# Layer 0's attention: every PSUM bank gets a fixed purpose, and the preparation of the next group moves behind the outputs and denominators of a step

## The chip, the cores and the metric

The kernel runs on one core of one Trainium2 chip. The metric is device time in microseconds (us), the median over runs. The engines are called by their names in the profile: PE is TensorE's matmul (PEld its weight load), ACT is ScalarE, DVE is VectorE, POOL is GpSimd, SP issues most transfers.

## The reference, cut to what matters

The whole is a decoder of two layers over x (32 sequences, 128 tokens, width 256, float32). Layer 0 is a self-attention, a cross-attention to a context with distance slopes, and a mixture of eight experts; layer 1 is a gated recurrence with an MLP, a second cross-attention and a quantised feed-forward.

```python
x = x + attn(layernorm(x))            # 16 heads of 16; keys and values from a latent of 64
x = x + xattn(layernorm(x), ctx)      # 16 heads, scores + slope * (kpos - qpos), masked, softmax with +1
x = x + moe(layernorm(x))             # top 2 of 8 experts, 256 -> 1024 -> 256
x = x + layer1_mixer_and_mlp(layernorm(x))
x = x + layer1_xattn(layernorm(x), ctx)
x = x + layer1_ffn(layernorm(x))      # quantised 256 -> 1024, conv over tokens, silu, 1024 -> 256
```

## The kernel before, in words

The residual x stays in SBUF. Layer 0's attentions run in one function, attention(), over 64 items: item ("a", g, i) is the self-attention of sequence i of group g (8 groups of 4 sequences), item ("b", g, i) the cross-attention of the same. All "a" items come first, then all "b" items. Step t of the loop at L641 walks the list slots (L636) and issues pieces of several items:

- a_scores (s_a): 32 matmuls of 32 rows into four banks, then four DVE maxima into nm (L444), one for each bank. a_maxima: two transposes (bank nm_a) and one DVE add, qS (L455). a_weights, one step later: scores again, transposed, into four banks st_a, and four ACT exponentials (L474). a_outs, two steps late: outputs and denominators in one bank, od_a; DVE takes a reciprocal (L497) and a product. merge, three steps late: output projection in one bank, y_a, added to x (L506).
- b_scores (s_b): 16 matmuls into four banks; 16 DVE operations add slope and mask and take a running maximum (L518); two small DVE operations give nan, the negated maxima (L524, L525); 16 ACT exponentials (L531) need nan; DVE sums half of the denominators (L536); POOL spreads their reciprocals (L544). b_turned, two steps late: 16 transposes into four banks et_b, copied three by ACT and one by DVE (L555). b_outs three steps late (od_b), b_dens two steps late (rd_b, copied by ACT L565), merge four steps late.
- ahead: one piece of the preparation of the item's successor group, four pieces per group. For "a": layer norm and transposed x (pt_a, copied by ACT L291); queries and latent (q_a, l_a); keys (k_a, eight ACT operations L356); values (v_a, L317). For "b": loads, mask and keys (k_b, four ACT operations L313) with the layer norm; transposed x (pt_b); queries (q_b, L402); values (v_b, L317).
- route(g), after the last b item of a group: layer norm, transposed x (pt_c), router logits (r_c), top two.

PE's instructions in these functions go through mm and turned, which keep them in program order. The framework orders the other engines' instructions ahead of time, by program order among those that it takes to be ready[...].

PSUM has 8 banks. Every tile is a whole bank, from one pool of 8 buffers: a new tile gets any bank that is free. This pool serves the whole kernel, the experts and layer 1 too.

Layer 1 is a list of pieces by step: PLAN gives the step of each piece of a unit (two sequences), and each unit starts 11 steps after the one before, so that pieces of several units share a step. The pieces that matter below are e_s and e_exp (scores s_e, read by one DVE maximum L1212 and two ACT exponentials L1217), f_flip (pt_f and rows_f), e_flip (pt_e), m_fc (f_m) and f_h (h_f):

```python
(45, "e_s"), (47, "e_exp"), (58, "f_flip"), (60, "f_h0"), (13, "d_v d_q2"),
(26, "m_fc0 m_fc1"), (36, "e_flip"),
```

Of the kernel before, what the change touches and what calls it, by code (L numbers as in the profile page):

```python
# [2 lines left out]

# [7 lines left out]
F32 = mybir.dt.float32  # L11
# [6 lines left out]
P = 128  # L18
# [57 lines left out]
def decoder(ctx: ExitStack, tc: tile.TileContext, a: dict, out: bass.AP):  # L76
# [11 lines left out]
    psp = ctx.enter_context(tc.tile_pool(name="ps", bufs=8, space=bass.MemoryType.PSUM))  # L88

    def bank(name, dt=F32):  # L90
        return psp.tile([P, 512 if dt == F32 else 1024], dt, tag="ps", name=name)
# [153 lines left out]
    def attention():  # L245
        with tc.tile_pool(name="pa", bufs=2) as pool, tc.tile_pool(name="pa1", bufs=1) as keep:
# [38 lines left out]
            def xposed(src, name):  # L285
                dst = pool.tile([P, 2, GS], F32, tag="xT", name=f"xT_{name}")
                for c in range(2):
                    pt = bank(f"pt_{name}_{c}")
                    for i in range(G):
                        turned(pt[:, i * P : (i + 1) * P], src[:, i, c * P : (c + 1) * P])  # L290
                    A.copy(dst[:, c, :], pt)  # L291
                return dst

            def feats(w, m, xT, name, kc=2, msz=P, rows=P):
                p = bank(name)
                for c in range(kc):
                    mm(p[:msz, :GS], w[:rows, c, m * msz : (m + 1) * msz], xT[:rows, c, :], c == 0, c == kc - 1)
                return p

            def toks(w, xT, i, name, kc=2, rows=P):  # L300
                p = bank(name)
                for c in range(kc):
                    mm(p[:, :D], xT[:rows, c, i * S : (i + 1) * S], w[:rows, c, :], c == 0, c == kc - 1)
                return p

            def key_halves(w, xT, name):


                kEO = pool.tile([P, 2, G, 2, S], F32, tag="kEO", name=f"kEO_{name}")
                for c in range(2):  # L310
                    p = feats(w, c, xT, f"k_{name}_{c}").rearrange("p (b k) -> p b k", b=G)
                    for e in range(2):
                        A.activation(kEO[:, c, :, e, :], p, AF.Copy, scale=pm[:, e : e + 1])  # L313
                return kEO

# [5 lines left out]
            def group_a(g):  # L321
# [13 lines left out]
                p = bank(f"l_{n}")  # L335
# [9 lines left out]
                pk = [bank(f"k_{n}_{h}").rearrange("p (c b k) -> p c b k", c=2, b=2) for h in range(2)]  # L345
# [16 lines left out]
                pv_ = [bank(f"v_{n}_{h}").rearrange("p (i d) -> p i d", i=2) for h in range(2)]  # L362
# [9 lines left out]
            def group_b(g):  # L372
# [32 lines left out]
                v = vEO[g % 2]  # L405
                for i in range(G):
                    value_halves(v, toks(W("b_v", 2), cT, i, f"v_{n}_{i}"), i)
                made["b", g] = qT, kEO, v, nd

            def score(b, i, m):  # L410

                qT, kEO, _, _ = made[b[:2]]
                sp = [bank(f"s_{m}_{r}") for r in range(4)]
                if b[0] == "a":
                    for c in range(2):
                        for e in range(2):
                            for r in range(4):
                                at = slice(32 * r, 32 * r + 32)
                                mm(
                                    sp[r][:, (2 * c + e) * S : (2 * c + e + 1) * S],  # L420
                                    qT[at, c, e, i * S : (i + 1) * S], kEO[at, c, i, e, :], True, True,
                                )
                    return [s.rearrange("p (c e k) -> p c e k", c=2, e=2) for s in sp]
                for c in range(2):
                    for r in range(4):
                        mm(
                            sp[r][:, c * 2 * S : (c + 1) * 2 * S],
                            qT[32 * r : 32 * r + 32, c, i * S : (i + 1) * S],
                            kEO[32 * r : 32 * r + 32, c, i].rearrange("p e k -> p (e k)"),
                            True, True,  # L430
                        )
                return [s.rearrange("p (j k) -> p j k", j=4) for s in sp]
# [16 lines left out]
            def a_maxima(b):  # L449
                i, m = b[2], f"a{b[1]}_{b[2]}"  # L450
                pt = bank(f"nm_{m}")
# [10 lines left out]
            def a_weights(b):  # L462
                g, i, m = b[1], b[2], f"a{b[1]}_{b[2]}"
                kEO, qS = made[b[:2]][1], state[b]
                st = [bank(f"st_{m}_{r}") for r in range(4)]
# [26 lines left out]
            def a_outs(b):  # L492
                m = f"a{b[1]}_{b[2]}"
                od = bank(f"od_{m}")
# [7 lines left out]
            def merge(b):  # L502

                xg, i = X[b[1]], b[2]
                y = toks(W(f"{b[0]}_o", 2), state.pop(b), 0, f"y_{b[0]}{b[1]}_{i}")
                V.tensor_tensor(xg[:, i, :], xg[:, i, :], y[:, :D], ALU.add)  # L506
# [40 lines left out]
            def b_turned(b):  # L547
# [3 lines left out]
                for r in range(4):  # L551
                    pt = bank(f"et_{m}_{r}")
# [5 lines left out]
            def b_dens(b):  # L558
                m = f"b{b[1]}_{b[2]}"
                et, den = state[b]  # L560
                p = bank(f"rd_{m}")
# [6 lines left out]
            def b_outs(b):  # L568
                m = f"b{b[1]}_{b[2]}"
                od = bank(f"od_{m}")  # L570
# [5 lines left out]
            def route(g):  # L576
# [7 lines left out]
                xT = xposed(xn, n)  # L584
                yield
                p3 = bank(f"r_{n}")[:, : G * NE].rearrange("p (b e) -> p b e", b=G)
# [47 lines left out]
            for _ in group_a(0):  # L634
                pass
            slots = (  # L636
                (a_scores, 0), (b_scores, 0), (ahead, 0), (a_weights, 1), (b_turned, 2),
                (a_outs, 2), (b_outs, 3), (merge, None), (b_dens, 2), (a_maxima, 0),
            )
            routing = []  # L640
            for t in range(len(items) + 4):  # L641
                for what, late in slots:
                    if what is merge:
                        for late in (4, 3):
# [7 lines left out]
                routing = [r for r in routing if next(r, routing) is not routing]  # L652
# [820 lines left out]
```

## Time and profile before

| | us |
|---|---|
| median of three runs | 2037.29 (2035.19 to 2041.46) |
| the profiled execution: time | 2041.52 |
| its span | 2039.4 |
| self-attention items with preparation of "a" groups, 56.88 to 255.09 | 198.2 |
| cross-attention items, from 290.40 to about 621 | 331 |
| experts, 740 to 1340 | 600 |
| layer 1, from 1340 | 699 |

The profile is of one execution; its span is 2.1 us shorter than its time. PE is busy for 89% of the span, DVE for 57%, ACT for 53%; but these are averages over stages: in the experts' stage PE has no gap and the others idle, in the cross-attention PE, ACT and DVE are all busy for about four fifths of the time. A matmul of 32 rows lasts 270 ns in the profile, though one starts about every 30 ns, so PE's busy share covers short gaps; PE's stalls are read here from the distance between the starts of successive tiles.

### The profile page before, as it was taken

How to read it: one execution, taken by the hardware profiler on the slowest of the kernel's cores; microseconds unless marked ns; L12 is line 12 of the kernel's file. 1: busy time of each engine (PE TensorE's matmuls, PEld its weight loads, DVE VectorE, ACT ScalarE, POOL GpSimd, SP SyncE). 2: the span in 40 equal slices, each digit the busy share in tenths (PEclk: the TensorE clock that was granted, in tenths of full speed). 3: DMA queues.
4: the chain of work that ended last, by engine and by line, in shares of the span. 5: the costliest groups of instructions: out<-in, count | busy, mean ns of one | idle time of the engine just before them, and what ended most of it. 6: DMA issues, size and time to landing. Idle time of an engine off the chain costs nothing.

```text
span 2039.4 us, 35437 instructions
## 1 busy us (share of the span) xinstructions
PE 1807.9 (89%) x13432; PEld 1477.4 (72%) x13432; DVE 1166.9 (57%) x3716; ACT 1080.8 (53%) x2584; POOL 421.9 (21%) x445
## 2 busy tenths in 40 slices
PE   6999999899986799999999995379989999999863
PEld 4777766676665478888888885268878887888752
DVE  6877667787777512101111111454677888888787
ACT  4454548888885422222222221235677777777662
POOL 4100000000000111111111102852333333333221
PEclk8999999998998899999999998689999999999976
DMA  4000010111002845555546553310000000000000
GB/s 155 3 2 3 8 38 22 33 33 52 16 19 75 325 174 180 202 192 187 211 173 210 183 189 120 87 49 11 11 11 27 16 17 21 27 16 21 27 11 21
DMA packets 51517, 162.13 MB, mean 79 GB/s; under 512 B 5392, under 2 KB 32144, under 8 KB 46224
## 3 DMA queue, kind: packets, MB, share of 16 engines
q1 hardware_dynamic: 44816, 141.99, 19.6%
q0 software_dynamic: 6528, 17.83, 3.1%
q8 instruction: 108, 1.77, 0.4%
q14 instruction: 65, 0.53, 0.1%
HBM read 132.80 MB, written 27.00 MB: 78 GB/s over the span
## 4 chain that ended last, share of the span: by engine, by line
PE 51%; DVE 26%; ACT 10%; POOL 6%; issue 4%; DMA 3%; SPq 0%; POOLq 0%; DVEq 0%; ACTq 0%
PE h L206 12%; PE y L206 12%; ACT sd_b L531 4%; PE od_a L206 3%; DVE top_f L1311 3%; DVE sd_b L518 2%; POOL z_f L1298 2%; PE st_a L206 2%; PE m_m L206 2%; PE et_b L209 2%; PE f_m L206 1%; DMA yr<-ys,slots 1%; DVE rd_a L497 1%; DVE nm L444 1%; PE q_a L206 1%
## 5 line engine op out<-in xcount | busy, mean ns | idle before, releaser
L820 ACT ACTIVATE hTs<-h,moe 128x256 f32<-128x256 f32 x288 | 136.3, 473 | 374.5 <-PE h L206 374.5
L206 PE MATMUL h<-xTs,moe 128*128 128x256 f32 x1152 | 254.7, 379 | 1.0 <-issue 1.0
L206 PE MATMUL y<-moe,hTs 128*128 128x256 f32 x1152 | 254.6, 379 | 0.0
L206 PEld LDWEIGHTS h<-xTs,moe 128*128 128x128 f32 x1152 | 218.7, 190 | 30.9 <-issue 1.2
L206 PEld LDWEIGHTS y<-moe,hTs 128*128 128x128 f32 x1152 | 216.2, 190 | 27.9
L531 ACT ACTIVATE sd_b<-sd_b,nan_b 128x128 f32<-128x128 f32 x512 | 173.8, 387 | 28.9 <-DVE nan_b L525 28.7
L795 POOL DMA_INDIRECT xr<-xs,who x72 | 68.3, 948 | 469.6 <-PE xs L209 426.8
L808 DVE COPY xTs<-xs 128x512 f32<-128x512 f32 x36 | 24.9, 690 | 236.1 <-PE xs L209 236.1
L832 DVE TENSOR_TENSOR yt<-y,moe 128x256 f32<-128x256 f32 x72 | 30.5, 424 | 215.7 <-PE y L206 215.7
L206 PE MATMUL m_m<-wd,sT_m 128*128 128x256 f32 x512 | 119.4, 381 | 0.0
L206 PE MATMUL f_m<-hT_m,wd 128*128 128x256 f32 x512 | 116.9, 383 | 0.0
L518 DVE CUSTOM_DVE_ANT_0 sd_b<-nd_b,s_b 128x128 f32<-128x128 f32 x512 | 113.0, 278 | 5.4 <-PE s_b L206 5.4
L1298 POOL TENSOR_TENSOR z_f<-z_f,e_f 128x508 f32<-128x508 f32 x64 | 70.7, 1104 | 197.3 <-ACT e_f L1296 110.1
L206 PEld LDWEIGHTS f_m<-hT_m,wd 128*128 128x128 f32 x512 | 96.4, 193 | 12.9 <-issue 0.5
L206 PEld LDWEIGHTS m_m<-wd,sT_m 128*128 128x128 f32 x512 | 95.8, 192 | 12.6 <-ACT sT_m L1158 0.2
L497 DVE RECIPROCAL rd_a<-od_a 128x256 f32<-128x256 f32 x32 | 56.0, 1751 | 63.2 <-PE od_a L206 63.2
L1282 ACT ACTIVATE z_f<-d_f,pv 128x256 f32<-128x256 f32 x128 | 70.3, 590 | 35.7 <-DVE d_f L1277 35.6
L544 POOL COPY dens_b<-den_b 128x256 f32<-128x256 f32 x32 | 12.8, 399 | 363.6 <-DVE den_b L542 202.3
L1292 DVE SCALAR_TENSOR_TENSOR z_f<-d_f,pv,z_f 128x254 f32<-128x254 f32 x128 | 64.1, 509 | 37.6 <-ACT z_f L1282 36.7
L474 ACT ACTIVATE et_a<-st_a 128x512 f32<-128x512 f32 x128 | 66.4, 614 | 27.6 <-PE st_a L206 27.6
L444 DVE TENSOR_REDUCE nm<-s_a 128x4 f32<-128x512 f32 x128 | 79.0, 680 | 2.6 <-PE s_a L206 2.6
L206 PE MATMUL s_b<-kEO_b,qT_b 32*128 32x256 f32 x512 | 53.3, 435 | 22.9 <-ACT kEO_b L313 17.0
(358 smaller groups left out, 4007.2 us busy)
## 6 DMA issues: line engine op xcount, KB each, us to landing
moe<-in_moe SPq DMA_DIRECT2D x36, 2180.0 KB, 8.6
ys<-yt SPq DMA_DIRECT2D x36, 256.0 KB, 2.3
ckv<-kv SPq DMA_DIRECT2D x8, 1024.0 KB, 5.2
kv_e<-ckv SPq DMA_DIRECT2D x16, 512.0 KB, 3.6
x<-in_x SPq DMA_DIRECT2D x8, 512.0 KB, 8.8
cT_b<-in_ctxT SPq DMA_DIRECT2D x8, 512.0 KB, 3.8
xs<-xn_c SPq DMA_DIRECT2D x8, 512.0 KB, 3.0
cT_k<-in_ctxT SPq DMA_DIRECT2D x8, 512.0 KB, 7.1
```

Of the source, the lines that this page charges most:

```text
L206: tc.keep_in_program_order(PE.matmul(out, lhsT=lhsT, rhs=rhs, start=start, stop=stop))
L444: V.tensor_reduce(nms[i % 2][:, at : at + 2 * (P - HD)].rearrange("p (e x) -> p x e", e=2)[:, :2, :], sp[r], AX.X, ALU.max, negate=True,)
L474: A.activation(et[:, r].rearrange("p j q -> p (j q)"), st[r], AF.Exp)
L497: V.reciprocal(rd, od[:, 2 * S :])
L518: V.tensor_tensor_reduce(sd[:, r, j, :], nd[:, i, :], sp[r][:, j, :], SLOPES[head(r, j)], -3e38, ALU.add, ALU.max, mx[:, 4 * r + j : 4 * r ...
L531: A.activation(sd[:, r, j, :], sd[:, r, j, :], AF.Exp, bias=nan[:, 4 * r + j : 4 * r + j + 1], accum_out=den[:, h : h + 1] if r % 2 else None,
L795: GP.indirect_dma_start(out=xr[h], out_offset=None, in_=xs[:, :], in_offset=bass.IndirectOffsetOnAxis(ap=who[:, q : q + 1], axis=0),)
L820: A.activation(hT[:, hc, :], p[:, :TS], AF.Relu, bias=b1[:, hc : hc + 1])
L1282: A.activation(o["z"][:, hc, :], o["d", k][:, j, :], AF.Identity, scale=cw[:, hc, 1:2], bias=cb[:, hc : hc + 1],)
L1292: V.scalar_tensor_tensor(z[:, :, 1:], d[:, j, :].rearrange("p (b t) -> p b t", b=U)[:, :, : S - 1], cw[:, hc, 0:1], z[:, :, 1:], ALU.mult, ...
L1298: GP.tensor_tensor(z[:, :, : S - 1], z[:, :, : S - 1], e.rearrange("p h (b t) -> p (h b) t", b=U)[:, :, 1:], ALU.add,)
L1311: V.tensor_reduce(o["top"][:, k, :], o["z"][:, 4 * k : 4 * k + 4, :].rearrange("p h t -> p t h"), AX.X, ALU.max, apply_absolute_value=True,)
```

## The change: what it does

1. bank() gets an argument at. The pool has eight tags of one buffer each, ps0 to ps7. With at the tile takes that bank; without it, tiles take the banks in turn, 0 to 7 and again, in program order. All bank() calls of the experts and of layer 1 are without at.
2. In attention() every tile has its bank: scores of both kinds 0 to 3, st_a and et_b 4 to 7, od 0, nm_a and rd_b 4, y 5, l_a 6, and the preparation's tiles 1 and 7 (PREP). The router's transposed x takes 6 and 3, its logits 6.
3. The cross-attention's values, four half-bank products, share two banks in place of four.
4. In a step, ahead moves from behind the scores to behind a_outs, b_outs and b_dens; b_dens moves ahead of merge. The router's piece moves from the end of the step to just before merge.

```diff
-    psp = ctx.enter_context(tc.tile_pool(name="ps", bufs=8, space=bass.MemoryType.PSUM))
-    def bank(name, dt=F32):
-        return psp.tile([P, 512 if dt == F32 else 1024], dt, tag="ps", name=name)
+    psp = ctx.enter_context(tc.tile_pool(name="ps", bufs=1, space=bass.MemoryType.PSUM))
+    turn = count()
+    def bank(name, dt=F32, at=None):
+        k = next(turn) % 8 if at is None else at
+        return psp.tile([P, 512 if dt == F32 else 1024], dt, tag=f"ps{k}", name=name)
...
+            PREP = 1, 7
-            def xposed(src, name):
+            def xposed(src, name, at=PREP):
...
-                    pt = bank(f"pt_{name}_{c}")
+                    pt = bank(f"pt_{name}_{c}", at=at[c])
...
-                p = bank(name)
+                p = bank(name, at=PREP[m])
...
+            def value_banks(n):
+                return [bank(f"v_{n}_{h}", at=PREP[h]).rearrange("p (i d) -> p i d", i=2) for h in range(2)]
...
-                p = bank(f"l_{n}")
+                p = bank(f"l_{n}", at=6)
...
-                pk = [bank(f"k_{n}_{h}").rearrange("p (c b k) -> p c b k", c=2, b=2) for h in range(2)]
+                pk = [bank(f"k_{n}_{h}", at=PREP[h]).rearrange("p (c b k) -> p c b k", c=2, b=2) for h in range(2)]
...
+                pv_ = value_banks(n)
                 for i in range(G):
-                    value_halves(v, toks(W("b_v", 2), cT, i, f"v_{n}_{i}"), i)
+                    toks(W("b_v", 2), cT, i, pv_[i // 2][:, i % 2, :])
+                for i in range(G):
+                    value_halves(v, pv_[i // 2][:, i % 2, :], i)
...
-                sp = [bank(f"s_{m}_{r}") for r in range(4)]
+                sp = [bank(f"s_{m}_{r}", at=r) for r in range(4)]
...
-                pt = bank(f"nm_{m}")
+                pt = bank(f"nm_{m}", at=4)
...
-                st = [bank(f"st_{m}_{r}") for r in range(4)]
+                st = [bank(f"st_{m}_{r}", at=4 + r) for r in range(4)]
...
-                od = bank(f"od_{m}")
+                od = bank(f"od_{m}", at=0)
...
+                y = bank(f"y_{b[0]}{b[1]}_{i}", at=5)[:, :D]
...
-                    pt = bank(f"et_{m}_{r}")
+                    pt = bank(f"et_{m}_{r}", at=4 + r)
...
-                p = bank(f"rd_{m}")
+                p = bank(f"rd_{m}", at=4)
...
-                xT = xposed(xn, n)
+                xT = xposed(xn, n, (6, 3))
...
-                (a_scores, 0), (b_scores, 0), (ahead, 0), (a_weights, 1), (b_turned, 2),
-                (a_outs, 2), (b_outs, 3), (merge, None), (b_dens, 2), (a_maxima, 0),
+                (a_scores, 0), (b_scores, 0), (a_weights, 1), (b_turned, 2), (a_outs, 2), (b_outs, 3),
+                (b_dens, 2), (ahead, 0), (merge, None), (a_maxima, 0),
...
                     if what is merge:
+                        routing = [r for r in routing if next(r, routing) is not routing]
...
-                routing = [r for r in routing if next(r, routing) is not routing]
```

More of the change, by code (lines that the diff above doesn't have):

```diff
@@ L2 @@
 from functools import partial
+from itertools import count
 import numpy as np
@@ L292, in xposed, with feats, toks @@
                 return dst
-            def feats(w, m, xT, name, kc=2, msz=P, rows=P):
-                p = bank(name)
-                for c in range(kc):
-                    mm(p[:msz, :GS], w[:rows, c, m * msz : (m + 1) * msz], xT[:rows, c, :], c == 0, c == kc - 1)
-                return p
[L300 to L304, printed above, removed]
+            def feats(w, m, xT, name):
+                p = bank(name, at=PREP[m])
+                for c in range(2):
+                    mm(p, w[:, c, m * P : (m + 1) * P], xT[:, c, :], c == 0, c == 1)
+                return p
+            def toks(w, xT, i, p):
+                for c in range(2):
+                    mm(p, xT[:, c, i * S : (i + 1) * S], w[:, c, :], c == 0, c == 1)
             def key_halves(w, xT, name):
@@ L361, in group_a @@
                 v = vEO[g % 2]
-                pv_ = [bank(f"v_{n}_{h}").rearrange("p (i d) -> p i d", i=2) for h in range(2)]
+                pv_ = value_banks(n)
                 for i in range(2):
@@ L405, in group_b @@
                 v = vEO[g % 2]
+                pv_ = value_banks(n)
                 for i in range(G):
-                    value_halves(v, toks(W("b_v", 2), cT, i, f"v_{n}_{i}"), i)
+                    toks(W("b_v", 2), cT, i, pv_[i // 2][:, i % 2, :])
+                for i in range(G):
+                    value_halves(v, pv_[i // 2][:, i % 2, :], i)
                 made["b", g] = qT, kEO, v, nd
@@ L504, in merge @@
                 xg, i = X[b[1]], b[2]
-                y = toks(W(f"{b[0]}_o", 2), state.pop(b), 0, f"y_{b[0]}{b[1]}_{i}")
-                V.tensor_tensor(xg[:, i, :], xg[:, i, :], y[:, :D], ALU.add)
+                y = bank(f"y_{b[0]}{b[1]}_{i}", at=5)[:, :D]
+                toks(W(f"{b[0]}_o", 2), state.pop(b), 0, y)
+                V.tensor_tensor(xg[:, i, :], xg[:, i, :], y, ALU.add)
             def b_scores(b):
@@ L569, in b_outs @@
                 m = f"b{b[1]}_{b[2]}"
-                od = bank(f"od_{m}")
+                od = bank(f"od_{m}", at=0)
                 outs(b, od, False)
@@ L583, in route @@
                 yield
-                xT = xposed(xn, n)
+                xT = xposed(xn, n, (6, 3))
                 yield
-                p3 = bank(f"r_{n}")[:, : G * NE].rearrange("p (b e) -> p b e", b=G)
+                p3 = bank(f"r_{n}", at=6)[:, : G * NE].rearrange("p (b e) -> p b e", b=G)
                 for i in range(G):
```

## The prediction

> **What bounds the kernel now.** I read the page's busy table and slices, then busy time by stage, then the waits of the cross-attention, then PE's timeline from one score tile to the next, which gives the length of each step.
>
> ```profile
> 56.88:157.59 100.71, 96.41 (x1730) 72.96 (x1729) 76.84 (x136) 52.27 (x105) 12.09 (x15) 1.00 0.01 3
> ...
> 371.62:595.75 224.13, 204.70 (x1761) 155.36 (x1760) 175.23 (x1035) 183.00 (x636) 17.45 (x29) 0.92 0.09 28
> ...
> 1460.00:1880.00 420.00, 399.74 (x2145) 341.08 (x2144) 349.93 (x909) 310.79 (x601) 149.46 (x138) 1.00 0.06 20
> ```
>
> Columns: length, then busy time of PE, PEld, DVE, ACT, POOL. Self-attention (first row) and layer 1 (last) are PE's; in cross-attention PE (91%), ACT (82%) and DVE (78%) are all loaded, so a step there lasts as long as its waits make it.
>
> Self-attention, one step:
>
> ```profile
> 185.57 2.48 DVE L444 TENSOR_REDUCE nm<-s_a 128x4 f32<-128x512 f32 x4
> 186.31 1.75 PE L206 MATMUL st_a<-qS_a,kEO_a 32*128 32x128 f32 x28 [0.57 <-DVE nm L444]
> ```
>
> st_a waits for banks that still hold this step's scores until DVE's maxima release them. By starts of s_a a group takes 7.64 (x transposed) + 10.01 (queries) + 7.85 (keys) + 8.07 (values) = 33.57 us in four groups and 31.97 in the two after 191 us. Unstalled pieces from the same starts: s_a 1.10, st_a 1.05, od_a 1.89, y_a 0.97, nm_a 0.31, together 5.32; the preparation adds 1.01, 4.69, 1.06, 1.06. So 29.1 us is PE's floor and 3 to 4.5 us are stalls.
>
> Cross-attention:
>
> ```profile
> 515.98 1.57 ACT L531 ACTIVATE sd_b<-sd_b,nan_b 128x128 f32<-128x128 f32 x5 [2.38 <-DVE nan_b L525]
> ...
> 521.41 0.67 ACT L313 ACTIVATE kEO_b<-k_b,cst 128x512 f32<-128x512 f32 x1
> ...
> 522.13 1.67 PE L206 MATMUL s_b<-kEO_b,qT_b 32*128 32x256 f32 x10 [2.15 <-ACT kEO_b L313]
> ...
> 523.00 0.29 DVE L518 CUSTOM_DVE_ANT_0 sd_b<-nd_b,s_b 128x128 f32<-128x128 f32 x1 [1.00 <-PE s_b L206]
> ```
>
> The 16 exponentials occupy ACT for 5.43 us (515.98 to 521.41). The last key copy stands behind them in ACT's list; the next scores wait for it, DVE for the scores, the next exponentials for DVE: a **serial loop**. Before, it closes once per group: steps with keys, transposed x, queries, values take about 11.0, 13.6, 11.0, 9.3 us. The others overlap DVE's slope operations with the previous exponentials, because in them the preparation stands directly behind the scores and ACT reads it before the exponentials begin.
>
> Layer 1:
>
> ```profile
> 1645.49 0.58 ACT L986 COPY xT_f<-pt_f 128x512 bf16<-128x512 bf16 x1
> 1645.95 0.39 ACT L1021 COPY rows_f_sb<-rows_f 128x256 f32<-128x256 f32 x1
> 1646.36 1.28 ACT L1217 ACT_TABLE_LOAD   x1
> 1647.65 0.37 ACT L1217 ACTIVATE at_e<-s_e,nm_e 128x128 f32<-128x128 f32 x1
> ```
>
> The second exponential that reads s_e ends at 1648.02; PE starts h_f0 at 1646.12. Before, that is no matter: h_f0 takes another bank.
>
> [...] behind today's stall of 4.4 us pt_b's matmuls take 421 ns against 273 for pt_a, and the stage's mean clock is 0.92.
>
> **The change part by part.** No instruction is added or taken away except that four value tiles become two. DMA issues keep their order on SP: a b group's three loads (L375, L379, L381) still precede the router's store in a step, and are needed a step later. POOL's share (L369, 0.76 us each; powers of 1 us) is 21% and keeps its order. These I cost at nothing; their cover is a whole step.
>
> *Self-attention.* The first half of st_a no longer meets the scores' banks. New waits, from the s_a start of a step as zero: od_a (bank 0) at 2.15 needs the first maximum, at 1.7. Preparation at 4.04 needs bank 7, free when st_a's four exponentials end: 2.1 + 2.07 = 4.2, so 0.1. The next s_a needs bank 0 from od_a's readers: 4.04 + 0.14 + 1.67 (reciprocal) + 0.4 (product) + 0.1 = 6.35, against PE's arrival at 6.33 to 6.38: nothing. Keys are worse: eight L356 at 0.469 between starts begin at 5.2; bank 1 comes free at 7.2 against s_a at 6.38 (stall 0.8), bank 7 at 9.05 against st_a at 8.2 (0.8). Behind these PE matmuls wait od_a, y_a and, through them, DVE. Queries: 10.01, all banks free. A group: 6.35 + 10.01 + (6.38 + 6.38 + 1.6) = 30.7. Gain 2.85 × 4 + 1.25 × 2 = 13.9; filling and the first b group's preparation, where 9.00 + 8.29 + 9.00 + 9.02 could become 3 × 8.86 + 6.33, give 1 to 2.5 more unless the kpos load (3.1 us of waiting there) holds. **Minus 15**, bounds 10 and 19.
>
> *Cross-attention.* PE now runs s_b 1.07, et_b 1.84, od_b 1.01, rd_b 0.53, and only then the preparation: at 4.45. Its first tile is complete at 4.45 + 1.77 = 6.2 (transposed x: 5.0). The exponentials are ready at 0.85 + 3.34 + 0.5 = 4.7 (as the trace has them: 522.13 to 523.00 for the first scores, 523.00 to 526.34 for 16 slope operations, two nan operations of 0.17 with their gaps). So ACT's list should have the exponentials first and bank 1's readers behind them, and s_b of the next step needs bank 1. The loop that closed once per group closes in every step: exponentials 5.43, P, 0.05 to PE, 0.85 for the first scores, 3.85 for slopes and nan: 10.2 + P, where P is bank 1's readers: keys 0.60 + 0.67, queries 0.65, values 0.29 + 0.37, transposed x 0.55; with the router's two copies behind it (bank 3) 1.9. Steps: 11.45, 12.1, 10.85, 10.85 = 45.2 us, without router 43.9. PE's own work in such a step is 7.5 to 10.7, so it hides[...]. Before, groups b0 and b1 (no router yet) take 39.95 and 41.27, b2 to b6 45.2, 44.9, 46.3, 43.3, 44.4. Difference: 3.9 + 2.6 + (226.0 − 224.1) = 8.4; in b7 the router's copy of bank 3 makes 8.14 into 11.0: 2.9. What is relieved: DVE's et_b copy no longer stands between the two nan operations waiting for PE, as it does now in the 13.6 us step. **Plus 11**, bounds −4 (ACT's list takes some copies early) and +20 (0.3 us more in every step from normalisation operations between slope and nan, as at 526.34).
>
> *The rest of the kernel, through "in turn".* I compared each PE start with the release of the tile eight before. Experts: 11 tiles per expert tile, every bank free over 2 us earlier: nothing. Before the experts, the eighth tile behind the token table waits for it: 0.5. Layer 1: behind s_e come v_d, q2_d, pt_f, rows_f, pt_e, f_m0, f_m1, and the eighth is h_f0. It now waits until 1648.02 in place of 1646.12: 1.9 us. PE's later idle of 0.91 before at_e gives that much back: plus 1.0 per unit period of 40 us; periods bound by PE: 420 / 40 = 10.5. (f_m0 takes o_f's bank, 0.4 late, inside the same wait.) **Plus 10.5**; bounds 0, if another ACT order puts the exponential first, and 20, if nothing is given back.
>
> Sum: −15 + 11 + 0.5 + 10.5 = **+7**. The profiled execution took 2041.5 (span 2039.4 and 2.1 around it) and would take 2048.5. It stands 4.2 above the median of 2037.3, from which I predict 2044.
>
> **The rivals.**
> *A, faster: the loop opens.* If ACT's list holds bank 1's reader ahead of the step's first L531, s_b runs ahead of the exponentials. Then a group is bound by PE (4 × 5.42, plus 3 × 3.54, 2.0 and 1.8 for preparation and router: 36) or ACT (four times 5.43 + 1.47 + 0.26, plus 6.7 of preparation: 35.3). Today's steps exceed PE's pieces by 0.35 (values, 9.3 against 8.96) to 2 (keys); I take 1.3, so about 41.5, and 44.8 − 41.5 = 3.3 gained in each of 7 groups, 23. With −15 and +10.5: 2010. For it: before, three of four key copies do precede the exponentials. Against it: their products come before 4.7 there, and at 6.2 now. It decides at that order alone: P out of the loop.
> *B, no change:* layer 1's list changes and s_e is read in time: −15 + 11 + 0.5, 2034. For it: only one table load separates the two readers' order. Against: v_d, pt_f and rows_f stand earlier in program order.
> *C, slower still:* a DVE operation that waits for PE lands between slope and nan in every step, 1 us × 28: 2072. For it: at 526.66 to 528.30 it does so now. Against: et_b now follows s_b directly.
>
> **How the numbers follow.** A measurement of this kernel tells 0.3%, 6 us, from no change. Forecast 0.44, A 0.29, B 0.20, C 0.07. The forecast's own range is 2032 to 2058. Faster: most of A and a third of B, 0.34; same: the rest of B and a third of the forecast, less A's gain, 0.22; slower 0.44. The range over the cases is 2006 to 2060.
>
> **What would show each step.** Self-attention: s_a to s_a near 6.4, 10.0, 7.2, 7.2, and PE's wait for nm gone from st_a. Cross-attention: s_b waiting for vEO, qT, xT and kEO in every step, L531 following each other at 10.8 or more. Layer 1: h_f waiting for at_e L1217, unit period 41. Wrong if L531's idle is ended by preparation copies ahead of it, if s_b waits for none of these, or if layer 1's period stays 40.0.

## The result, and the profile after

The changed kernel takes **2121.2 us** (median of 4 runs, 2116.3 to 2123.4) against 2039.4 for the kernel before in the same comparison (4 runs, 2035.2 to 2042.7): a ratio of **1.0399**, 95% interval 1.0380 to 1.0419. I had predicted 2044, range 2006 to 2060. The direction was right, the size far off: 82 us are lost where I had 7.

All stage lengths below are read the same way, from starts of tiles on PE in one profiled execution: the first s_a, the first s_b, the tile "counts" that begins the token table, the first y_m of layer 1, and the end of PE's last matmul, which lies 4.3 us ahead of the end of the span before and 5.0 us ahead of it after.

| kernel | first s_a at | self-attention | cross-attention | table and experts | layer 1 | time of that run |
|---|---|---|---|---|---|---|
| before | 28.4 | 262.0 | 366.1 | 663.5 | 715.0 | 2041.5 |
| after | 34.3 | 254.2 | 439.7 | 661.5 | 723.5 | 2120.1 |
| difference | +5.9 | −7.8 | **+73.6** | −2.0 | +8.5 | +78.6 |
| predicted | 0 | −15 | +11 | +0.5 | +10.5 | +7 |

The stages of after in busy time, in the order of the first three rows of the prediction and with the same columns; the third last is PE's granted clock. The first row holds three groups of self-attention, the second groups b2 to b6, the third ten periods of layer 1 (the prediction's row had ten and a half):

```profile
63.69:160.69 97.00, 90.47 (x1729) 70.79 (x1728) 77.51 (x136) 52.62 (x105) 11.95 (x15) 1.00 0.01 3
384.70:655.24 270.54, 215.81 (x1762) 160.93 (x1761) 178.94 (x1034) 181.54 (x631) 17.13 (x29) 0.88 0.08 25
1571.80:1978.50 406.70, 382.37 (x2045) 327.99 (x2044) 338.91 (x859) 294.75 (x565) 140.92 (x128) 0.99 0.06 19
```

The same five cross-attention groups take 270.5 us instead of 224.1. ACT's and DVE's busy time there hardly changed (181.5 and 178.9; 183.0 and 175.2 before), PE's share fell from 91% to 80%, and PE's clock from 0.92 to 0.88. So no engine got more work (PE's 11 us more of busy time come with the lower clock): the stage is waiting. PE's waits in that stretch, each with its total, count and longest:

```profile
PE s_b L211 <- ACT xT_c L300: 23.5, 5, 4.7
PE s_b L211 <- ACT vEO L328: 13.2, 5, 2.9
PE s_b L211 <- ACT kEO_b L320: 12.3, 5, 3.6
```

The scores wait for a preparation copy on ACT in three of the four steps of each group, as the prediction's serial loop says. In the fourth, ACT has copied the queries out of bank 1 by 590.0, and s_b follows at 590.45 behind PE's own work. A turn of the loop is named here after the preparation whose copies stand behind its exponentials. The turn with the transposed x, from the timeline of all engines (start, length, instruction, idle before it and what ended it):

```profile
574.90 0.39 ACT L546 ACTIVATE sd_b<-sd_b,nan_b 128x128 f32<-128x128 f32 x1
575.28 0.56 ACT L300 COPY xT_b<-pt_b 128x512 f32<-128x512 f32 x1
...
575.75 1.06 ACT L300 COPY xT_c<-pt_c 128x512 f32<-128x512 f32 x2
576.86 2.07 PE L211 MATMUL s_b<-kEO_b,qT_b 32*128 32x256 f32 x10 [4.70 <-ACT xT_c L300]
578.13 0.29 DVE L533 CUSTOM_DVE_ANT_0 sd_b<-nd_b,s_b 128x128 f32<-128x128 f32 x1 [2.25 <-PE s_b L211]
...
578.86 3.67 PE L214 MATMUL et_b<-cst,sd_b 128*128 128x128 f32 x16
...
582.57 0.69 DVE L570 COPY et_b<-et_b 128x512 f32<-128x512 f32 x1 [1.02 <-PE et_b L214]
583.18 0.16 DVE L539 TENSOR_SCALAR nan_b<-mx_b 128x16 f32<-128x16 f32 x1
583.38 0.18 DVE L540 SCALAR_TENSOR_TENSOR nan_b<-mx_b,nan_b 128x16 f32<-128x16 f32 x1
583.59 0.69 ACT L546 ACTIVATE sd_b<-sd_b,nan_b 128x128 f32<-128x128 f32 x2 [1.28 <-DVE nan_b L540]
```

The last exponential of a step ends, then the copies of the banks that s_b wants, then s_b, then the slopes, then nan, then the next exponentials. The copies keep their place in ACT's list: bank 7's transposes end at 569.78 (a modelled end), and its copy starts at 575.28, behind the sixteenth exponential. That is the chain that I had drawn, with one difference: in this turn bank 1's copy ran ahead of the exponentials (569.38 to 569.97), and what s_b waits for is the router's copy of bank 3. Two pieces are longer than I put them. From s_b's resumption to the first slope it takes 1.27 us here, not 0.85; and the slopes end at 581.54, but nan comes 1.6 us later, because DVE's list has the fourth et_b copy ahead of it, and that copy waits for PE, whose 16 transposes take 3.67 us. In the fourth step, where PE did not stop, the same 16 take 1.97.

Layer 1's predicted wait is there, and its period went from 40.0 to 40.4 or 42.1, on average 40.7:

```profile
PE h_f L211 <- ACT at_e L1232: 21.5, 10, 3.1
```

### The profile page after: what moved, and what is told of

Read it like the earlier page. It is cut to its first block, busy times and chain, and to the rows that moved or that the text cites. A ratio compares the mean times of both kernels' runs of the same rounds, so it can differ in the third digit from the quotient of the medians.

```text
span 2118.2 us, 35387 instructions
## 1 busy us (share of the span) xinstructions
PE 1819.9 (86%) x13432; PEld 1490.5 (70%) x13432; DVE 1178.3 (56%) x3716; ACT 1084.8 (51%) x2584; POOL 419.9 (20%) x445
## 4 chain that ended last, share of the span: by engine, by line
PE 59%; DVE 18%; ACT 13%; POOL 3%; issue 3%; DMA 3%; SPq 0%; POOLq 0%; DVEq 0%; ACTq 0%
PE h L211 12%; PE y L211 12%; ACT sd_b L546 6%; PE m_m L211 4%; PE f_m L211 3%; PE od_a L211 3%; PE et_b L214 3%; DVE top_f L1326 3%; PE s_b L211 2%; DVE sd_b L533 1%; ACT kEO_a L367 1%; PE y_m L211 1%; PE ck L190 1%; PE k_e L211 1%; PE vv_e L211 1%
## 5 line engine op out<-in xcount | busy, mean ns | idle before, releaser
L211 PE MATMUL f_m<-hT_m,wd 128*128 128x256 f32 x512 | 121.3, 393 | 2.8 <-DVE x L1361 2.8
L211 PE MATMUL s_b<-kEO_b,qT_b 32*128 32x256 f32 x512 | 61.2, 487 | 59.5 <-ACT xT_c L300 23.5
L214 PEld LDWEIGHTS et_b<-cst,sd_b 128*128 128x128 f32 x512 | 76.5, 178 | 20.4 <-issue 12.6
L211 PEld LDWEIGHTS s_b<-kEO_b,qT_b 32*128 32x128 f32 x512 | 34.3, 221 | 80.3 <-ACT xT_c L300 25.5
L214 PE MATMUL et_b<-cst,sd_b 128*128 128x128 f32 x512 | 86.1, 338 | 5.2 <-ACT xT_b L300 2.7
```

Source lines behind the costliest of these rows:

```text
L211: tc.keep_in_program_order(PE.matmul(out, lhsT=lhsT, rhs=rhs, start=start, stop=stop))
L214: tc.keep_in_program_order(PE.transpose(out, in_, ident if by is None else by))
```

## The experiments

Most of these kernels ran once (the kernel before took 2037 to 2042 beside them), so no difference of under 6 us in a whole time is used. The diffs show only the lines that matter ("..." stands for the rest), with remarks behind #. The stages, in the columns of the table above:

| kernel | first s_a | self | cross | table, experts | layer 1 | time |
|---|---|---|---|---|---|---|
| order_alone | 28.6 | 253.7 | 367.9 | 663.3 | 714.0 | 2033.7 |
| banks_alone | 35.4 | 409.9 | 573.9 | 661.1 | 723.8 | 2410.5 |
| prep67 | 34.2 | 254.1 | 392.8 | 658.3 | 729.1 | 2075.7 |
| et_act | 34.7 | 253.1 | 440.4 | 657.9 | 726.7 | 2119.0 |
| nan_first | 34.2 | 254.0 | 428.4 | 658.6 | 729.5 | 2110.9 |
| prep67_nan | 35.4 | 254.1 | 411.1 | 660.3 | 729.6 | 2096.7 |
| exps_late | 34.3 | 254.2 | 403.2 | 661.6 | 729.5 | 2088.8 |
| rest_free | 29.8 | 257.6 | 433.7 | 663.5 | 715.5 | 2106.4 |
| et45 | 33.7 | 254.1 | 457.8 | 659.3 | 729.3 | 2140.3 |
| od6_router6 | 34.8 | 296.6 | 426.6 | 657.5 | 724.8 | 2148.2 |

### Order or banks?

**order_alone** takes the kernel before and moves only the preparation and the router in a step; tiles still come from the free pool.

```
-  (a_scores, 0), (b_scores, 0), (ahead, 0), (a_weights, 1), (b_turned, 2),
-  (a_outs, 2), (b_outs, 3), (merge, None), (b_dens, 2), (a_maxima, 0),
+  (a_scores, 0), (b_scores, 0), (a_weights, 1), (b_turned, 2), (a_outs, 2), (b_outs, 3),
+  (b_dens, 2), (ahead, 0), (merge, None), (a_maxima, 0),
```

> The kernel before with the new order of a step alone; all tiles still from one free pool of eight banks. ACT's list then has the same order as in the changed kernel (exponentials L531 ahead of the step's preparation copies), so this run tells order from banks. Theory L (the next scores share bank 1 with a preparation tile, whose reader stands behind the 16 exponentials): from the pool a score tile follows, eight tiles back, a tile of the weights transposed or the outputs, not a preparation tile; so s_b waits for no preparation copy, slope operations overlap exponentials, a cross-attention group takes 38 to 43 us instead of 54.65, and the whole 2000 to 2030. Theory O (the order itself, preparation behind outputs and exponentials ahead of the copies, makes the loop, whatever the banks): a group stays at 52 to 55 and the whole at 2100 to 2120. Layer 1's period should be that of before, 40.0, in both.

**banks_alone** takes the changed kernel and puts the order of before back.

> The changed kernel's banks with the order of before in a step, except in two of the 64 steps (the first of the last self-attention group and the first cross-attention step), which keep the new order because there the keys would hold bank 7 against the very st_a that frees their SBUF buffer. ACT's list then has bank 1's copy ahead of the exponentials and bank 7's behind them in steps with keys, queries and values. Theory L: s_b waits only for bank 1, so the loop is open: a group of 40 to 45 us, though PE now stands behind the slope operations of r=1 for bank 1, 1 to 2 us a step. Theory O: also fast, since the order is the old one; so this run tells L from a third, B (banks as such, scores and outputs sharing bank 0 and fewer free banks, make it slow): 50 or more. Self-attention: preparation behind the scores waits for the second maximum in bank 1, so a group of 33 to 35 in place of 32.3. Layer 1 keeps the wait of the changed kernel, period near 40.9. Whole: 2035 to 2065 under L.

Order alone: self-attention 253.7, the whole gain of the changed kernel and no less; cross-attention 367.9, and groups b2 to b6 take 44.1 to 47.3 us each, 45.3 on average (44.8 in the kernel before). That is not the 38 to 43 expected, but far from 52. Theory O, that the order makes the loop, is out. In these five groups no s_b waits for a copy. PE's waits in two and a half of them:

```profile
PE et_b L209 <- ACT vEO L317: 5.4, 3, 1.8
PE et_b L209 <- DVE mx_b L518: 4.7, 2, 2.4
PE et_b L209 <- ACT kEO_b L313: 3.0, 3, 1.0
```

The wait has not gone: a tile of transposed weights, one place later in PE's list, now waits for the keys' and values' copies, and for less long. Which tile lay in a score tile's bank before it, by the banks of the compiled programs, tells why s_b is free. Of the 80 score tiles of groups b2 to b6, 25 follow a preparation or router tile in the changed kernel, at least one in every step; in order_alone 9 do, and in the kernel before 15.

Banks alone was worse than any theory had it: I expected 2035 to 2065 and it took 2410. In cross-attention a preparation tile waits for slopes (bank 1), and a tile of transposed weights for copies behind exponentials (bank 7). PE's waits in groups b2 to b6, one line of each kind:

```profile
PE et_b L214 <- ACT kEO_b L320: 23.1, 5, 4.9
PE v_b L211 <- DVE mx_b L533: 18.4, 5, 3.7
```

Self-attention, for which I had expected 33 to 35 us a group, takes 51 to 54 in seven of eight. PE's longest waits in one group of it:

```profile
PE s_a L211 <- DVE oT_a L513: 6.2, 5, 1.3
PE st_a L211 <- ACT kEO_a L367: 3.4, 1, 3.4
```

The next s_a stands right behind od_a, whose bank 0 it needs, and must wait for the reciprocal and the product; in the changed order the preparation covers that. Each of the four preparation tiles waits 1.3 us for a maximum besides, as expected. So the banks need the order: in cross-attention they cost 207.8 us with the old one (573.9 − 366.1) and 71.8 with the new (439.7 − 367.9). In self-attention they gain nothing over the order alone (254.2 and 253.7).

### Which bank closes the loop?

**prep67** moves the preparation of b groups off the scores' banks:

```
+            PREP_B = 6, 7      # xposed, feats and value_banks of group_b, and its keys
...
-                y = bank(..., at=5)[:, :D]
+                y = bank(..., at=5 if b[0] == "a" else 4)[:, :D]
...
-                xT = xposed(xn, n, (6, 3))      # route
+                    pt = bank(f"pt_{n}_{c}", at=5)      # its two halves one step apart
...
```

> The changed kernel with one thing moved in cross-attention: the preparation tiles of b groups in banks 6 and 7 (not 1 and 7), so that none shares a bank with scores; the router's transposed tiles go one by one through bank 5, a step apart, and y_b to bank 4, for the same reason. Order, ACT's list and everything else stay. Theory L: s_b no longer waits for kEO, qT, xT or vEO; the third transposed weight tile (bank 6) does instead, half a step later, while slopes already run; the clock stays up; a group of 38 to 43 us, the whole 2020 to 2040. Theory O: no change, group 52 to 55, whole 2100 to 2120.

Cross-attention falls from 439.7 to 392.8: 47 of the 72 us that the banks cost. s_b waits no more. But a group still takes about 48 us, and the loop has moved, to the transposed weights: the second tile waits for the router's copy in bank 5, the third for the keys' in bank 6 (PE's waits in two groups):

```profile
PE et_b L214 <- ACT xT_c L606: 9.2, 4, 3.5
PE et_b L214 <- ACT kEO_b L322: 5.3, 4, 2.2
```

**exps_late** keeps the banks and splits b_scores, so that the exponentials are written behind the preparation; ACT's list then has at most ten of them ahead of the copies of keys, x, queries and values, not sixteen.

```
-  (b_dens, 2), (ahead, 0), (merge, None), (a_maxima, 0),
+  (b_dens, 2), (ahead, 0), (b_exps, 0), (merge, None), (a_maxima, 0),
```

> The changed kernel, with the exponentials written behind the preparation in the program: ACT's list then has the preparation copies of a step after two to ten exponentials and not after all sixteen; banks and PE's order stay. Theory L (s_b waits for bank 1's reader behind the exponentials): s_b comes 3 to 5 us earlier in the steps with keys, transposed x, queries and values, a group of 43 to 49, the whole 2040 to 2080. If the loop is something else: group 53 or more, the whole above 2105.

The last three full groups take 51.2 each, the stage 403.2, 36.5 less; the group is longer and the whole a little slower than expected, because in the turn with the transposed x s_b still waits for the router's copy of bank 3, which ACT has behind all sixteen (6.5 us in two groups):

```profile
PE s_b L211 <- ACT xT_c L300: 6.5, 2, 3.2
```

It is the test nearest to the cause, since it changes neither a bank nor PE's list: the same banks cost half as much when their reader stands ahead of most of the exponentials.

**od6_router6** has the router's halves one by one in bank 6 (and od_a in bank 6, for self-attention):

```
-                od = bank(f"od_{m}", at=0)      # a_outs
+                od = bank(f"od_{m}", at=6)
...
-                xT = xposed(xn, n, (6, 3))      # route
+                    pt = bank(f"pt_{n}_{c}", at=6)      # its two halves one step apart
...
```

> The changed kernel with two edits in stages that lie apart. Self-attention: od_a in bank 6 and not in bank 0. If the queries' step is long because od_a waits 1.28 us for the maxima of the scores in bank 0, which DVE reads only behind a layer norm, that step falls from 11.15 to 10.0 or less, and the s_a starts that wait for oT_a (0.4 a time) go, too: the stage from 254 to 240 to 247. If the step is DVE's own length, nothing moves. Cross-attention: the router's transposed tiles one by one in bank 6, none in bank 3. If bank 3 is a cause of its own, the queries' step loses its 6.3 us of waiting (a group near 49); if bank 1 alone closes the loop, s_b there waits for xT_b in its place, 0.5 to 1.5 us sooner: a group of 53 to 54.5 and the stage at 428 to 438.

Cross-attention 426.6: taking the router out of bank 3 is worth 13 of the 73.6. Bank 3's own share may be larger, because the router's tile in bank 6 now stops a tile of transposed weights (PE's waits in two groups):

```profile
PE et_b L214 <- ACT xT_c L604: 6.4, 2, 3.2
```

Self-attention went the other way, to 296.6. My expectation had overlooked that st_a of the same step has just filled bank 6, so od_a waits for its exponentials every time, 1.7 us (PE's waits in 150 us):

```profile
PE od_a L211 <- ACT et_a L488: 28.0, 17, 1.7
```

Bank 0 was the better of the two places; the one wait that it costs per group is shown further down.

### What stands between slopes and nan?

**et_act**: all four et_b copies on ACT.

```
-                    (V.tensor_copy if r == 3 else A.copy)(et[:, r] ..., pt)
+                    A.copy(et[:, r] ..., pt)
```

> The changed kernel with all four copies of the transposed weights on ACT, so that no DVE operation waiting for PE stands between slopes and nan. If that copy is what the 7.2 us per group between slopes' end and exponentials cost (I had costed it 1.8), a group falls by 5 to 49.5 and the whole by 36 to about 2085. If the transposes on PE themselves come too late (they start when s_b resumes, at half the clock), ACT's fourth copy, which stands ahead of the exponentials, ends about when DVE's did, and only nan's 0.5 to 0.9 us a step is gained: a group of 51.5 to 53, the whole 2098 to 2110.

Nothing gained, 440.4. With the copy gone, the planner put the outputs' product oT_b between the two nan operations, and that waits for PE, too:

```profile
583.40 0.42 DVE L588 TENSOR_TENSOR oT_b<-od_b,rd_b 128x256 f32<-128x256 f32 x1 [2.19 <-PE od_b L211]
```

**nan_first** pins both behind nan in DVE's list, **prep67_nan** does it in prep67.

```
+                ready[0] = tc.keep_in_program_order(V.scalar_tensor_tensor(nan, mx, ...))
...
+                    if r == 3:      # et_b's fourth copy
+                        behind_nan(ins)
...
+                behind_nan(V.tensor_tensor(oT ..., od[:, : 2 * S], state[b][1], ALU.mult))
```

> The changed kernel with two DVE operations that wait for PE (the fourth copy of the transposed weights and the outputs' product oT_b) pinned behind nan in DVE's list, so that nothing stands between the slopes and nan; banks and PE's order stay. Rival C (such an operation delays nan in every step; et_act had merely let oT_b take the copy's place): the 7.2 us a group between the end of the slopes and the exponentials fall to 2.5 to 3.5, less where ACT's own copies of et_b, which stand ahead of the exponentials, wait for PE at half clock; a group of 50 to 51.5, the whole 2085 to 2100. If the DVE operations only fill time that the loop through bank 1 would lose anyway: a group above 53.5, the whole above 2110.

> Both at once: preparation of b groups in banks 6 and 7, router in 5, y_b in 4, and nan ahead of the DVE operations that wait for PE. Theory: in prep67 the loop only moved (exponentials, preparation copy, bank 6, third weight transposed, its DVE copy, nan, exponentials: 47.9 us a group); with the DVE operations behind nan it is cut, what is left is exponentials 5.5, copies 1.2, a transpose and its ACT copy 1.8, so about 9 us a step: a group of 36 to 41 and the whole 2005 to 2035. If the loop is not the cause of what is left, the group stays at 46 to 48 and the whole at 2065 to 2080.

nan_first: 428.4, 11.3 less, half of the smallest gain expected. In the changed kernel ACT's own three et_b copies stand ahead of the exponentials, too, and wait for the same transposes (3.67 us behind the stop of 4.70, at a clock of 0.50). That would explain why most of the 5.4 us a group that the copy seems to cost is lost anyway; no run tests it apart. prep67_nan is a miss: 411.1, worse than prep67. In it ACT's list has rd_b's copy behind the exponentials, and y_b, which I had moved to bank 4, waits for it (8.2 us in 100).

**et45** tries to leave no bank for the loop: transposed weights in banks 4 and 5 in turn, y_b in the second half of rd_b's tile. **exps_behind_rd** pins the exponentials behind rd_b's copy besides.

```
-                    pt = bank(f"et_{m}_{r}", at=4 + r)
+                    pt = bank(f"et_{m}_{r}", at=4 + r % 2)
...
-                y = bank(f"y_{b[0]}{b[1]}_{i}", at=5)[:, :D]
+                y = merged[0][:, D:]            # the other half of rd_b's tile
```

> prep67_nan with its preparation banks 6 and 7 taken away from the weights transposed, too: et_b's four tiles go through banks 4 and 5 in turn, y_b lies in the second half of rd_b's bank (so that it waits for no ACT copy of rd_b, as it did 8.2 us in 100 in prep67_nan), the router's tiles one by one in bank 5. A preparation tile of b groups then shares its bank with another preparation tile alone. Theory L (what costs is that a copy on ACT, behind 5.5 us of exponentials, holds a bank that PE's list needs early in the next step): PE waits for no preparation copy, exponentials follow each other every 9 to 10 us, a group of 36 to 41 and the whole 2010 to 2040. Rival (the stage is bound by what each engine has to do in the fixed order, so any plan of banks ends near 48): 47 to 51, the whole 2070 to 2095.

> et45 showed that one ACT copy behind the exponentials (rd_b, 0.35 us, whose bank y_b shares) is enough to close the loop. Here the exponentials stand behind rd_b's copy in ACT's list, so that no bank that PE's list needs before the next preparation is read behind them; the rest as in et45 (preparation in 6 and 7, transposed weights in 4 and 5, nan ahead of DVE operations that wait for PE), and outside cross-attention as in rest_free (free pool for the rest, group 0's preparation in other banks). Theory L: PE waits for no copy behind the exponentials; a step takes what PE has to do, 8 to 10 us; a group of 36 to 42 us, cross-attention 300 to 345, the whole 1970 to 2015. If the stage stays above 366 (the kernel before), then a loop of another kind or the fixed order itself is left and theory L explains only part of the loss.

Both missed by far: 457.8 and 430.5 (2098.6 us, ratio 1.0284, 1.0267 to 1.0301). PE's waits name the bank each time, in two groups of et45 and then of exps_behind_rd:

```profile
PE rd_b L211 <- ACT rd_b L601: 19.9, 8, 4.3
```

```profile
PE et_b L217 <- ACT xT_c L633: 9.3, 4, 3.5
PE et_b L217 <- ACT et_b L595: 9.3, 6, 3.5
```

In et45 the tile that waits is y_b (it bears rd_b's name), for a copy of 0.35 us from other columns of its bank. No run tells whether the bank sets this wait or that both lie in one tile. In exps_behind_rd the second transposed tile, in bank 5, waits for the router's copy, and the third, in bank 4, for the copy of the first; both copies stand behind exponentials. Each plan took one reader out of the way and put another one into it. That supports the mechanism (an ACT copy behind 5.5 us of exponentials, and a bank that PE's list wants early), in banks 1, 3, 4, 5 and 6; it does not support my belief that a plan of eight fixed banks without it was at hand. The rival of et45's expectation, that the order binds the stage near 48 whatever the banks, does not fit order_alone's 45.3. Both kernels also take 82 us from the last group's first scores to the table (the kernel before 61, the changed one 73); the reason stays open.

### Start and layer 1

**rest_free** gives everything behind the attention a free pool again, and group 0's keys banks 2 and 3, its values 4 and 5.

```
+    fixed.close()      # after attention()
+    psp.append(ctx.enter_context(tc.tile_pool(name="psr", bufs=8, space=bass.MemoryType.PSUM)))
...
-    pk = [bank(f"k_{n}_{h}", at=PREP[h]) ...]
+    pk = [bank(f"k_{n}_{h}", at=PREP[h] if g else 2 + h) ...]
...
+                pv_ = value_banks(n, PREP if g else (4, 5))
```

> The changed kernel with two parts undone in stages that lie apart: after the attention all tiles come from a free pool of eight banks, as before; and group 0's preparation ahead of the loop puts its keys in banks 2 and 3 and its values in 4 and 5 (not all in 1 and 7). Layer 1: if its slower period (40.4 and 42.1 for 40.0) is the second exponential of s_e, eight tiles behind, it returns to 40.0 and the stage to 714 to 716, minus 9; if it comes from elsewhere, it stays at 723 to 729. Start: if the 6 us are value tiles that wait for the eight key copies in the same two banks, the first s_a comes at 28.5 to 30 instead of 34.3. The cross-attention keeps its 54.6. Whole: 2103 to 2108.

Layer 1 is back at 715.5 and its period at 40.0; h_f waits for xT_f again, as it did before the change with the same 9.1 us, and no longer for at_e:

```profile
PE h_f L214 <- ACT xT_f L1004: 9.1, 10, 3.1
```

That confirms the cause and the size. Cross-attention, whose banks and order are those of the changed kernel, takes 433.7, not 439.7; 5.5 of the 6 us fall into its last group, and why stays open. A difference of that size in one group of one execution should not be read as an effect. The start did not come back: s_a begins at 29.8, but its last 26 matmuls only at 33.0, since now the keys held the scores' banks 2 and 3; first s_b 287.4 instead of 288.5. In the changed kernel most of the six us are the value tiles (0.7 is that DVE's wait for x ends at 11.77 there, at 11.07 before):

```profile
30.48 1.22 PE L211 MATMUL v_a<-wab,lT_a 64*128 64x256 f32 x2 [5.96 <-ACT kEO_a L367]
```

The key copies themselves cannot start before 28.5 (27.8 in the kernel before), because the DVE operation that makes their bias is so late; the first values then wait for four of them, the last for all eight, and s_a stands behind.

### What can be kept

**order_a_only** is the kernel before with the new order in self-attention alone; **pool_nan** pins nan in it as nan_first does. **best2** and **best2_nan** use fixed banks in self-attention (with od_a in bank 6); from the first cross-attention step on they have the free pool and the order of before.

> The kernel before (one free pool of eight banks) with the new order of a step in self-attention alone; cross-attention keeps the old order. If the self-attention's gain is the order's, as order_alone says (253.7 for 262.0), it is had here whole, and cross-attention stays at 366: the whole 2027 to 2032. If the gain in order_alone came from what follows (the first cross-attention group's preparation in the new order), the self-attention stays above 258 and the whole at 2034 to 2040.

> The new order of a step in self-attention alone, free pool, timed against the kernel before: 8 to 10 us less, 2027 to 2033, 0.4 to 0.5%.

> order_a_only (free pool, new order in self-attention alone; 2032.0, ratio 0.9968) with nan ahead of the two DVE operations that wait for PE. If such an operation is on the path with the free pool, too, as best2_nan's stage says (360.2 for 366.3): cross-attention 357 to 361 and the whole 2024 to 2029, ratio 0.993 to 0.996. If the stage's 6 us come back later: 2030 to 2034, ratio 0.996 to 0.998.

> Fixed banks and the new order in self-attention alone, with od_a in bank 6 and group 0's preparation in other banks; from the first cross-attention step on the free pool of eight banks and the order of before. If fixed banks gain in self-attention beyond the order alone (255.4 in order_a_only): self-attention 240 to 248, cross-attention 362 to 368, the whole 2015 to 2026. If they add nothing, the whole 2028 to 2034.

> best2 with nan ahead of the DVE operations that wait for PE. In the kernel before such an operation stands there once or twice in four steps and costs 0.6 to 2 us; if that is on the path, 5 to 15 us less than best2; if the step is bound elsewhere, within 3 us of it.

order_a_only: self-attention 255.4 and 253.7 in two profiles, cross-attention 363.7 and 363.8, and timed **2032.0 us, ratio 0.9968** (0.9952 to 0.9985): faster than both kernels, by 8 us over the one before. pool_nan: 2033.3, ratio 0.9965 (0.9953 to 0.9977), the same; the cross-attention was 366.5 in its profile. best2 and best2_nan miss, 2079.4 and 2079.8 (ratios 1.0190 and 1.0202): they carry od_a in bank 6, which cost 42 us in od6_router6; their self-attention is 303.7 and 303.5. In this pair pinning nan did go with a shorter cross-attention, 360.2 for 366.3, but not with a shorter whole time. So with scores that get their banks in time, the DVE operation in front of nan costs nothing that a whole time shows.

## Why the prediction was wrong

**The loop: right mechanism, wrong terms.** The wait of s_b, its place in ACT's list and its closing in every group were as written, though it closes in three steps of four. The failed step is the sum "exponentials 5.43, P, 0.05, 0.85, 3.85: 10.2 + P". Over a group of four steps (557.50 to 612.13) the pieces are:

| piece, four steps | predicted | measured |
|---|---|---|
| exponentials | 21.7 | 22.1 |
| bank readers P, and to PE | 4.7 | 4.6 |
| s_b resumes to first slope | 3.4 | 7.2 |
| slopes | 13.6 | 13.6 |
| end of slopes to exponentials | 1.8 | 7.1 |
| sum | 45.2 | 54.6 |

The measured exponentials include the last one's accumulator read. That P fits is in part luck: in the turn with the queries the 1.3 us counted end with PE's own work, 0.5 us behind the copy.

*To the first slope:* 0.78, 1.27, 3.13 and 2.01. I took the 0.85 of one step with keys for all. In the turn with the queries DVE has the router's choice of experts in front (from 589.6 to 593.6), in the turn behind it the router's layer norm, and behind two of the stops the clock is halved (0.50). Before the change such operations ran beside the previous exponentials or in between the slopes (in one turn the router's choice from 497.13 to 500.78, the exponentials to 497.72, the slopes from 498.58); in a serial loop they lie on the path. I had priced normalisation operations at 0.3 us a step in the upper bound and left them out of the sum; the router's choice I had not priced at all.

*To the exponentials:* 1.45, 2.05, 1.14 and 2.51. I wrote that DVE's et_b copy "no longer stands between the two nan operations"; it stands ahead of them in every step. et_b follows s_b on PE at once, as I said, but s_b is late itself, and behind two of the stops PE's clock is 0.50. In three of the four turns the product oT_b stands between the two nan operations as well, and in two an ACT copy stands between nan and the exponentials. That was rival C, to which I gave 0.07 and 28 us; nan_first puts its own share at 11.

*The clock.* The sum has no term for it: that PE's pauses in the loop would cost no more clock than the stop of 4.4 us that I read in the kernel before was my estimate. The gaps are 2.16, 4.70, 0 and 2.91 us, and after both long ones, with the clock at 0.50, the 16 transposes take 3.67 instead of 1.97. The 4.4 us were misread, too: PE's pauses there are 1.40 and 2.15 us, with six score matmuls between, and the clock is 0.50 from 522.58 on:

```profile
518.63 1.35 PE L206 MATMUL s_b<-kEO_b,qT_b 32*128 32x256 f32 x6 [1.40 <-DVE et_b L555]
```

In each of the last three full groups the clock is halved behind two of the four gaps. What that cost alone was not tried: no experiment here keeps PE busy while it waits.

By groups, b0 lost 5.2, b1 9.8, b2 to b6 together 46.4 and b7 12.2 us; predicted were 3.9, 2.6, 1.9 and 2.9. The table explains b2 to b6; what b1 and b7 lost beyond the prediction, 16.5 us, was not taken apart.

**Self-attention: a term too good.** −7.8, not −15. Keys and values together are as written (14.5 for 14.36), transposed x takes 6.63 for 6.35. "Queries: 10.01, all banks free" failed; the step takes 11.15 in four groups of six:

```profile
103.43 1.47 DVE L165 TENSOR_SCALAR xn_a<-x,mv_a,rs_a 128x256 f32<-128x256 f32 x3
...
105.37 1.86 DVE L458 TENSOR_REDUCE nm<-s_a 128x4 f32<-128x512 f32 x3
106.08 0.64 PE L211 MATMUL od_a<-et_a,vEO 128*32 128x128 f32 x16 [1.28 <-DVE nm L458]
```

od_a in bank 0 needs the first maximum. I had it at 1.7 us after s_a; in this step DVE has three rows of the next group's layer norm in front of it, and the first of the maxima starts at 2.6. In order_alone the free pool leaves od_a the same wait of 1.24, and the step takes 11.65; bank 6 brought the longer wait for the exponentials. So no run shows the step without a wait. The start, +5.9, was not in my sum: I did not follow the first group's preparation, which has only three banks. order_alone shows the rest of the view to be mistaken, too: the gain that I ascribed to the banks' separation (st_a free of the scores) is had by the order alone.

**Layer 1: right.** +10.5 predicted, +8.5 measured, the wait of h_f for at_e as named, undone by rest_free. (The other kernels with fixed banks to the end have 723.8 to 729.6 there, so the term is 9 to 15.) **Table and experts:** +0.5 for −2.0, nothing that a single execution tells.

**The rivals.** A (23 us faster once the loop is open) is not seen as a size: with no s_b waiting, order_alone's stage is 367.9, about what it was before, though there the transposed weights wait in its place. B falls with layer 1.

## What to carry to other kernels

When two tiles share a bank, ask in whose list the first one's reader stands, and what is queued ahead of it: here a 0.6 us copy behind 5.5 us of exponentials stopped all of PE's list for 2.2 to 4.7 us. When a loop turns serial, everything on its engines between its links goes onto the path, including what was hidden before (another stage's operations, a slower clock: the two pieces around the slopes took 14.3 us a group where I had 5.2), so take the sum over every step of a period, not from one step. The free pool did better here than any of the fixed plans tried in cross-attention and layer 1, and as well in self-attention. Half of a combined change, the order in self-attention, is worth its 0.3% alone.

## What the runs showed of the hardware

The length of a pause alone does not tell what the clock does. In the changed kernel the granted clock stayed at 1.00 behind a pause of 2.16 us and was 0.50 behind one of 2.91 us; in the kernel before it was 0.50 behind 2.15 us with 1.40 shortly ahead (all as the profile shows them, with modelled ends of matmuls). In these two traces the halved stretches that begin and end within the cross-attention last 3.41, 6.83 or 10.24 us, that is one, two or three times 3.41, called slots here. In the changed kernel such stretches begin at 521.59, 548.90, 576.20, 603.51 and 630.82, each 27.3 us or eight slots behind the one before. A group of 54.63 us is sixteen slots, so in the last groups each pause returns to the same place in them, and its returns are not separate trials. Slots with the pauses of 2.16 and 2.91 and the slot behind the second, in the changed kernel (length, then PE's busy time; the third last number is the clock):

```profile
562.56:565.96 3.40, 1.74 (x20) 1.38 (x21) 1.84 (x13) 2.75 (x7) 0.40 (x1) 1.00 0.02 5
600.10:603.50 3.40, 1.20 (x5) 0.47 (x3) 1.81 (x6) 3.40 (x17) 0.00 (x0) 1.00 0.00 0
603.52:606.90 3.38, 2.69 (x17) 1.88 (x18) 2.46 (x14) 1.17 (x6) 1.40 (x2) 0.50 0.00 0
```

The slot with the pauses of the kernel before, and the one behind it:

```profile
519.18:522.57 3.39, 1.24 (x13) 0.80 (x12) 1.68 (x6) 3.39 (x14) 0.40 (x1) 1.00 0.02 5
522.59:525.98 3.39, 3.39 (x21) 2.65 (x14) 2.98 (x29) 2.01 (x5) 0.00 (x0) 0.50 0.00 0
```

The pause of 2.16 us (562.06 to 564.22) lies across the start of a slot, and PE is busy for 1.74 us in the slot that holds most of it; in the other two slots it is busy for 1.20 and 1.24, and the clock is halved at their end. What decides is not shown, and the busy time of a slot does not tell it either: once, at 498.69 in the kernel before, the clock is halved behind a slot in which PE did not pause (busy for 3.41 of 3.41 us) and ran the router's matmuls, 8 columns wide, and a score tile.
